# Moving the key and value projections of a decoder layer's attention behind a block of query work

## The chip, the cores and the metric

The kernel runs on one core of a Trainium2 chip. The metric is the device time of one execution in microseconds (us). A core has five engines that run their own instruction streams in order and wait for each other through semaphores: TensorE (PE in the profile; its weight loads are listed as PEld), VectorE (DVE), ScalarE (ACT), GpSimd (POOL) and SyncE (SP). SP does little but issue DMA transfers; ACT issues some too. An instruction that waits holds back all that stands behind it in the same engine's stream.

## The reference

One decoder layer on 1024 tokens of 512 features, in float32. Attention has 32 query heads in 8 groups of four; a group shares one key and one value head of 128 features. Then come a layer norm with the residual, a gated feed-forward network of 1792 hidden features behind an RMS norm, and a second layer norm.

```python
q, k, v = x @ wq, x @ wk, x @ wv             # 32, 8, 8 heads of 128
q = q * cos + rotate_half(q) * sin           # the same for k
scores = einsum('bhtd,bhsd->bhts', q, repeat(k, 4)) / sqrt(128)
att = softmax(where(tril, scores, -inf))
x = layernorm(x + einsum('bhts,bhsd->bhtd', att, repeat(v, 4)) @ wo)
n = rms_norm(x) * ln_w
x = layernorm(x + (silu(n @ gate_w.T) * (n @ up_w.T)) @ down_w.T)
```

## The kernel before, in words

Line numbers (L) are those of the kernel before; the profile names instructions by them. All matmuls are issued in one helper, L145, so the profile tells them apart by their tiles.

**Slots.** Attention is a loop over the groups g = 0 to 7, within a group over eight blocks of 128 tokens in the order i = 7, 1, 5, 3, 4, 2, 6, 0 (p = 0 to 7 counts them), and within a block over four slots of 32 tokens. A slot treats 32 tokens of all four heads at once, so 128 rows, and is named by its place t = 4i + b among the tokens: a group runs through the slots 28 to 31, 4 to 7, 20 to 23, 12 to 15, 16 to 19, 8 to 11, 24 to 27, 0 to 3. `s23` below is the score matmul of slot 23. `scores` (L604) does one slot: TensorE multiplies queries with the keys up to the slot's end (tile `s`, up to two matmuls), VectorE adds the mask and takes the minimum (L623), ScalarE takes the exponential (L643), VectorE the reciprocal of the sum (L647), ScalarE scales (L648), VectorE transposes 32x32 blocks into the tile `turned` (L651). The short slots' remainder is cleared by POOL (L638).

**Behind a block.** After a block's fourth slot `gather` (L683) issues 16 DMAs on SP (L701), which complete the transposition into `moved`. Then, as deferred pieces (`Late`, L816), TensorE multiplies with the values (tile `o`), ScalarE copies (`oT`, L884), and pairs of blocks are multiplied with `wo` in a Strassen scheme: seven products (tile `y`), sums of the operands on POOL (`os`, L785 to L788), sums of the results on VectorE (L807). `y_0` to `y_3` are the four pairs of a group; a pair's last products run in the next group. `load_wo` (L320) issues the two halves of a group's `wo`, `wo_0` and `wo_1`, on SP (L327), when the group before has ended `y_3`; `weigh_wo` (L332) then forms sums of them on POOL (L340 to L343: u1, u3 in place, u2, u4). `y_0` uses `wo_0`, then `wo_1`, then u4, u1, u2 and both halves again.

**Projections.** `project_two` (L492) projects the keys or the values of two groups at a time, or two query heads, for half of the tokens or all, again by seven Strassen products of two matmuls each, which `run` (L975) deals out between slots. `Early` (L900) holds these pieces. What may run at a slot is bounded by a pace (`pace`, `must`) that follows the slot's number, with the constants `KNOWN` and `MOST`. `steps` lists all weight loads in order of use, and `load(s)` issues step s on SP (L249); key weights are scaled by POOL (L258); `weigh(s)` forms sums of the weights on POOL (L293 to L295). Pairs of weights, `wo` halves among them, share four buffers.

**The unit.** In the groups 1 to 5 the queries of the next group (2 to 6, `UNITS`) are projected in one stretch without slots, after p = 4 (`MIDDLE`), by Strassen's scheme nested in itself. This is `Unit` (L1133): seven outer products in the order `INNER` = 1, 2, 6, 7, 5, 3, 4, each a generator `stages` (L1042) with stages that interleave with the neighbours'. A stage ends in ScalarE copies (L1053), and the last in VectorE additions (L1088). `weigh_unit` (L298) forms the outer sums of the query weights on POOL (L306 to L308) and `inner_weights` the inner ones (L1024 on). The sums of the input are kept in HBM and fetched by DMAs that ScalarE issues (`fetch`, L1022; x1, x2, x6 in `prepare` during the four slots of p = 4; x7, x5 at the start of `run`, x3 and x4 within). x6 lies in the part of `turned` that p = 5 to 7 use later. The last stages of the last product run behind the following slots (`ending`). At the end of `run` two loads are issued.

**Rotary work.** A projected query or key tile is rotated later: `rotate_later` (L430) queues three chores, two half multiplications with the sine (L438) and one with the cosine (L443) on VectorE, the last followed by an addition on POOL (L444). `scores` draws one chore per slot.

**Order.** Matmuls, and instructions passed through `ordered` (L1017), keep the program's order on their engine. All others are ordered by a list scheduler, engine by engine, when the kernel is built; the order in which an SP load and a block's gathers come out depends on it.

## Time and profile before

| what | before |
|---|---|
| median of two runs | 1355.7 us (1353.36 and 1358.04) |
| profiled execution | 1354.13 us, span 1352.3 (1.8 us lie around it) |
| mean clock granted to TensorE | 0.972 of full |
| DMA, mean over the span | 102 GB/s, 137.66 MB |
| one SP gather DMA, from issue to landing | about 2.1 us; issues 0.634 us apart |
| `wo` half, query, key, value pair weights, to landing (median) | 5.3, 4.3, 3.9, 3.5 us |
| a unit group's length | about 140.5 us (L145's gaps at 291.78, 431.60, 574.06, 714.73 and 854.01) |

The span is the time from the first to the last instruction. The page's groups give the line, the engine, the operation with its tiles, the shape, the number of instructions, then the busy time and the mean in ns, and last the idle time of the engine ahead of these instructions with what ended most of it ("<-"). A row of the timeline gives the start, the length, the engine, the line, the operation and tiles, how many instructions of one kind follow each other, and, in brackets, the idle time before with its releaser. SPq rows are DMA issues on SP. The table of stretches has, for each window in us: its length, the busy time (and instructions) of PE, PEld, DVE, ACT and POOL, the mean granted clock, the DMA share and GB/s.

### The profile page before, as it was taken

The page shows a single profiled execution, that of the slowest core. Times are in us where ns is not written, and L with a number is a line of the kernel's source. Part 1 is how long each engine was busy: PE and PEld are TensorE (multiplying, and loading weights), DVE is VectorE, ACT ScalarE, POOL GpSimd, SP SyncE. Part 2 cuts the span into 40 slices and gives each one's busy share as a digit, 9 for nine tenths or more (in the row PEclk, how much of TensorE's full clock was granted, in tenths as well). Part 3 has the DMA queues.
Part 4 walks back from the last instruction along what each step waited for, and adds up shares of the span by engine and source line. Part 5 has one row for each costly group of instructions (what it writes and reads, how often), then busy time and mean ns, then how long its engine had stood idle before and what let it go on. Part 6 is the DMA issues. An engine that isn't in the chain of part 4 may idle for free. (4 is left out here: it accounts for less than half of the span.)

```text
span 1352.3 us, 15887 instructions
## 1 busy us (share of the span) xinstructions
PE 1252.4 (93%) x4556; PEld 824.1 (61%) x4556; DVE 966.2 (71%) x1926; ACT 568.2 (42%) x1210; POOL 595.9 (44%) x897
## 2 busy tenths in 40 slices
PE   9999998889988998899898979897999999999998
PEld 5645664655564755555565756554465666886787
DVE  5867885598748863888488747884866577788765
ACT  0443443445334543444344444543546515765100
POOL 5556425342443334234533254333332095969422
PEclk9999999989988998999898999898999999999999
DMA  7344435424552455135622562344354421122000
GB/s 256 68 105 145 130 79 167 137 66 93 145 154 53 99 138 164 55 72 143 183 68 66 127 173 85 75 96 108 91 121 105 115 76 38 42 70 103 2 31 32
DMA packets 90102, 137.66 MB, mean 102 GB/s; under 512 B 18976, under 2 KB 55584, under 8 KB 90016
## 3 DMA queue, kind: packets, MB, share of 16 engines
q1 hardware_dynamic: 83968, 116.33, 33.3%
q10 hardware_dynamic: 6048, 20.32, 4.6%
q8 instruction: 37, 0.61, 0.2%
q14 instruction: 49, 0.40, 0.1%
HBM read 55.58 MB, written 5.77 MB: 45 GB/s over the span
## 5 line engine op out<-in xcount | busy, mean ns | idle before, releaser
L643 ACT ACTIVATE p<-s,low 128x928 f32<-128x928 f32 (+31 forms) x256 | 179.1, 700 | 308.8 <-DVE low L623 276.3
L145 PE MATMUL o<-moved,v 128*128 128x512 f32 x550 | 264.1, 617 | 4.0 <-DVE sums L807 2.0
L623 DVE CUSTOM_DVE_ANT_0 s<-s,mask 128x928 f32<-128x928 f32 (+31 forms) x256 | 179.6, 702 | 93.2 <-PE s L145 92.4
L145 PE MATMUL s<-k,queries 128*128 128x512 f32 (+15 forms) x576 | 206.8, 475 | 36.9 <-ACT p L643 36.9
L648 ACT ACTIVATE p<-p,share 128x928 f32<-128x928 f32 (+31 forms) x256 | 186.5, 734 | 119.0 <-DVE share L647 119.0
L651 DVE STREAM_TRANSPOSE turned<-p 128x1024 f32<-128x1024 f32 (+7 forms) x244 | 184.4, 771 | 60.1 <-ACT p L648 46.3
L145 PEld LDWEIGHTS s<-k,queries 128*128 128x128 f32 x576 | 107.4, 195 | 131.0 <-issue 77.5
L145 PEld LDWEIGHTS o<-moved,v 128*128 128x128 f32 x550 | 107.0, 199 | 113.7 <-issue 101.6
L145 PE MATMUL y<-wo,oT 128*128 128x256 f32 x428 | 108.0, 386 | 10.7 <-DMA wo<-wo 8.0
L444 POOL TENSOR_TENSOR queries<-queries,q_b 128x512 f32<-128x512 f32 x52 | 66.8, 1284 | 92.8 <-DVE queries L443 72.6
L145 PEld LDWEIGHTS y<-wo,oT 128*128 128x128 f32 x428 | 80.7, 193 | 36.6 <-issue 22.7
L638 POOL MEMSET p<- 128x96 f32 (+2 forms) x192 | 26.9, 152 | 166.5 <-DVE turned L651 125.4
L438 DVE TENSOR_TENSOR q_b<-queries,sin 64x512 f32<-64x512 f32 x104 | 94.5, 909 | 3.2
L807 DVE TENSOR_TENSOR sums<-y,sums 128x512 f32<-128x512 f32 x112 | 67.5, 614 | 12.4 <-PE y L145 11.4
L647 DVE RECIPROCAL share<-total 128x1 f32<-128x1 f32 x256 | 39.7, 155 | 44.8 <-ACT p L643 41.4
L884 ACT COPY oT<-o 128x512 f32<-128x512 f32 x58 | 33.7, 580 | 89.1 <-PE o L145 88.9
L145 PE MATMUL s<-kT,queries 128*128 128x512 f32 (+8 forms) x192 | 68.6, 466 | 1.4 <-ACT p L643 1.4
L145 PEld LDWEIGHTS s<-kT,queries 128*128 128x128 f32 x192 | 35.8, 190 | 36.9 <-issue 28.9
L145 PE MATMUL y<-u,os 128*128 128x256 f32 x224 | 54.8, 381 | 1.9 <-POOL os L785 0.8
L145 PE MATMUL a<-x,k 128*128 128x256 f32 x156 | 51.5, 414 | 2.2 <-ACT b L1053 2.2
L643 ACT ACTIVATION_READ_ACCUMULATOR p<-s,low 128x1 f32 x256 | 49.4, 193 | 0.0
L145 PEld LDWEIGHTS y<-u,os 128*128 128x128 f32 x224 | 42.1, 190 | 11.2 <-issue 3.1
(398 smaller groups left out, 2317.8 us busy)
## 6 DMA issues: line engine op xcount, KB each, us to landing
x<-inner_x ACTq DMA_DIRECT2D x30, 512.0 KB, 4.7
moved<-turned SPq DMA_DIRECT2D x112, 128.0 KB, 2.4
moved<-turned SPq DMA_DIRECT2D x128, 112.0 KB, 2.2
moved<-turned SPq DMA_DIRECT2D x112, 96.0 KB, 2.2
moved<-turned SPq DMA_DIRECT2D x112, 80.0 KB, 3.8
wo<-wo SPq DMA_DIRECT2D x16, 512.0 KB, 5.3
moved<-turned SPq DMA_DIRECT2D x128, 64.0 KB, 2.0
wq<-wq SPq DMA_DIRECT2D x14, 512.0 KB, 4.3
```

The costliest lines, as they stand in the source:

```text
L145: tc.keep_in_program_order(nc.tensor.matmul(*args, **kw))
L438: nc.vector.tensor_tensor(alike(b[0], dst)[to], dst[of], alike(sin[:, ts], dst)[of], ALU.mult)
L444: nc.gpsimd.tensor_tensor(dst, dst, alike(b[0], dst), ALU.add)
L623: extreme = nc.vector.tensor_tensor_reduce(out=s[:, :n], in0=s[:, :n], in1=mask[:, T - n :], scale=1.0, scalar=MASKED, op0=ALU.add, op1=AL ...
L638: cleared = nc.gpsimd.memset(p[:, n:full], 0.0)
L643: nc.scalar.activation(p[:, :n], s[:, :n], AF.Exp, bias=low, scale=-1.0, accum_out=total)
L647: nc.vector.reciprocal(share, total)
L648: last_of_all = nc.scalar.activation(p[:, :n], p[:, :n], AF.Copy, scale=share)
L651: nc.vector.transpose(x[:, :, :, b, :].rearrange("p b j q -> p j b q"), p[:, :full].rearrange("p (j b k) -> p j b k", b=B, k=Q),)
L807: pin(nc.vector.tensor_tensor(to, out, to, ALU.add))
L884: nc.scalar.copy(oT, o)
```

## The change

Four things move, all in groups with a unit or next to one.

- The loads: where the group's queries are a unit's, its two loads of query weights are listed ahead of the key or value pair in `steps`; `projections` takes its step accordingly. The unit's end issues the key or value weights and the first query weights of the next unit; `project_two`'s end issues the second, and its last step calls `weigh_unit` for the unit one group on.
- The keys and values of two groups are projected in slots behind the unit (p = 5 to 7) instead of from the group's first slot on. In the first half nothing of `Early` is dealt out (the limit is 0), and the pace in the second counts slots from p = 5, with `KNOWN` 9. `weigh(3 * (g + 1))` stands at p = 5 instead of `weigh(3 * (g + 1) + 1)` at p = 6.
- The unit: the outer products begin at other places, the fetches of x7 and x5 are issued in its first two iterations, and the last product's next-to-last stage runs inside it, so that one stage instead of two is left in `ending`.
- Six rotary chores, those of the first two query heads that the unit has completed, are drawn in its last three iterations (`rotate`), with x6's room as scratch in place of a `rope_b` buffer.

```diff
@@ -96,7 +96,7 @@
 UNITS = range(2, KV - 1)
 UNIT = 24.5
 MIDDLE = 4
-KNOWN = 12
+KNOWN = 9
 INNER = (1, 2, 6, 7, 5, 3, 4)
 
 
@@ -265,8 +265,9 @@
 
         steps = [("v", 0, 1)]
         for g in range(KV - 2):
-            steps.append(("kv"[g % 2], g + 1, g + 2))
-            steps += [("q", 2 * n, 2 * n + 1) for n in (2 * g + 2, 2 * g + 3)]
+            two = ("kv"[g % 2], g + 1, g + 2)
+            four = [("q", 2 * n, 2 * n + 1) for n in (2 * g + 2, 2 * g + 3)]
+            steps += four + [two] if g + 1 in UNITS else [two] + four
         steps += [("k", KV - 1)] + [("q", n, n + 1) for n in (HEADS - 4, HEADS - 2)]
 
         def load(s):
@@ -432,19 +433,24 @@
             ts = slice(even * W, (even + 1) * W)
             b = []
 
-            def half(to, of):
+            def half(to, of, room=None):
+                if not b and room is not None:
+                    b.append(room)
                 if not b:
                     b.append(ap.tile([P, W], F32, tag="rope_b", name=f"{name}_b{even}"))
-                nc.vector.tensor_tensor(
+                return nc.vector.tensor_tensor(
                     alike(b[0], dst)[to], dst[of], alike(sin[:, ts], dst)[of], ALU.mult
                 )
 
-            def whole():
-                nc.vector.tensor_tensor(dst, dst, alike(cos[:, ts], dst), ALU.mult)
+            def whole(room=None):
+                ins = nc.vector.tensor_tensor(dst, dst, alike(cos[:, ts], dst), ALU.mult)
                 nc.gpsimd.tensor_tensor(dst, dst, alike(b[0], dst), ALU.add)
+                return ins
 
             low, high = slice(0, 64), slice(64, P)
-            chores[when].extend([lambda: half(low, high), lambda: half(high, low), whole])
+            chores[when].extend(
+                [lambda room=None: half(low, high, room), lambda room=None: half(high, low, room), whole]
+            )
 
         def chore(behind=None):
 
@@ -571,14 +577,14 @@
                     done(0, 1)
                     if s > 1:
                         load(s + 2)
-                    if s % 3 == 1 and s // 3 + 1 in UNITS:
+                    if s % 3 == 0 and s // 3 + 1 in UNITS:
                         weigh_unit(s // 3 + 1)
                 yield 1
 
         def projections(g):
 
 
-            s, pieces = 3 * (g - 1) + 1, []
+            s, pieces = 3 * (g - 1) + (3 if g in UNITS else 1), []
             if g < KV - 1:
                 pieces.append((PAIR * 2, project_two(s)))
             else:
@@ -1135,7 +1141,7 @@
 
             def __init__(self, g):
                 self.g, self.rooms, self.weights, self.begun = g, {}, [], []
-                self.last = None
+                self.last, self.turns = None, 0
 
             def fetch(self, k, room):
                 self.rooms[k] = room
@@ -1181,6 +1187,14 @@
                     self.v = ap.tile([P, 3, W // 2], F32, tag="os", bufs=1, name=f"v{g}")
                     self.begin()
 
+            def rotate(self, most):
+                room = self.rooms[INNER[2]]
+                for _ in range(most):
+                    if chores[0]:
+                        with_room = (room[:, :W], room[:, W:])[self.turns // 3 % 2]
+                        ordered(chores[0].popleft()(with_room))
+                        self.turns += 1
+
             def begin(self):
                 n = len(self.begun)
                 k = INNER[n]
@@ -1192,28 +1206,37 @@
             def run(self):
                 nonlocal now, quiet
                 g, begun = self.g, self.begun
-                for k in (7, 5):
-                    ordered(self.fetch(k, piece(f"x{k}_{g}")))
                 next(begun[0])
+                self.begin()
                 for n in range(1, len(INNER)):
-                    self.begin()
-                    for back in (1, 0, 2, 1):
-                        if back <= n:
-                            next(begun[n - back])
+                    next(begun[n - 1])
+                    next(begun[n])
+                    if n < 3:
+                        k = INNER[n + 2]
+                        ordered(self.fetch(k, piece(f"x{k}_{g}")))
+                    if n == 1:
+                        self.begin()
+                    if n > 1:
+                        next(begun[n - 2])
+                    next(begun[n - 1])
                     if n > 1 and self.last:
                         self.last()
                         self.last = None
                     self.weigh()
                     if n in (2, 3):
                         ordered(self.fetch(INNER[n + 3], self.rooms[INNER[n - 2]]))
+                    if n > 3:
+                        self.rotate(2)
+                    if 1 < n < len(INNER) - 1:
+                        self.begin()
                 next(begun[-1])
                 next(begun[-2])
-                now += UNIT - 2
+                next(begun[-1])
+                now += UNIT - 1
                 quiet = False
-                ending.extend([begun[-1], begun[-1]])
-                s = 3 * (g - 1) + 1
-                load(s + 3)
-                load(s + 4)
+                ending.append(begun[-1])
+                load(3 * g)
+                load(3 * g + 1)
 
         def step_out(l):
             nonlocal now
@@ -1300,8 +1323,8 @@
                     load_wo(g)
                 if g + 1 in UNITS and p == MIDDLE:
                     unit = Unit(g + 1)
-                if g + 1 in UNITS and p == MIDDLE + 2:
-                    weigh(3 * (g + 1) + 1)
+                if g + 1 in UNITS and p == MIDDLE + 1:
+                    weigh(3 * (g + 1))
                 if g == 0 and p >= NT // 2:
                     for k in INNER[2 * p - NT :][: 2]:
                         with tc.issue_after(cleared.ins):
@@ -1342,10 +1365,12 @@
                         continue
                     end_some()
                     if g + 1 in UNITS and p <= MIDDLE:
-                        pace = early.total * min(1, done / KNOWN)
-                        must = early.total - MOST * max(0, KNOWN + 1 - done)
+                        run(g, due, early, 0, 0, LEAST, 0)
+                    elif g + 1 in UNITS:
+                        behind = done - (MIDDLE + 1) * B
+                        pace = early.total * min(1, behind / KNOWN)
+                        must = early.total - MOST * max(0, KNOWN + 1 - behind)
                         run(g, due, early, pace, must, LEAST)
-                        end_some()
                     elif g < KV - 2:
                         pace = early.total * min(1, passed / (slots - EARLIER))
                         must = early.total - MOST * max(0, slots - EARLIER - done)
```

## The prediction

> **What bounds the kernel now.** First the page: who is busy, and what TensorE waits for.

> ```profile
> PE 1252.4 (93%) x4556; PEld 824.1 (61%) x4556; DVE 966.2 (71%) x1926; ACT 568.2 (42%) x1210; POOL 595.9 (44%) x897
> ...
> L145 PE MATMUL s<-k,queries 128*128 128x512 f32 (+15 forms) x576 | 206.8, 475 | 36.9 <-ACT p L643 36.9
> ...
> L145 PE MATMUL y<-wo,oT 128*128 128x256 f32 x428 | 108.0, 386 | 10.7 <-DMA wo<-wo 8.0
> ```

> TensorE (PE) has 100 us idle in 1352.3, and matmuls run in program order: whatever one of them waits for adds to the time. The change works in groups 1 to 5, which have a unit. TensorE's timeline of one such stretch (group 2, a unit from 373 to 402) shows the gaps in brackets:

> ```profile
> 344.47 1.45 PE L145 MATMUL s<-k,queries 128*128 128x512 f32 x4
> ...
> 356.15 1.89 PE L145 MATMUL y<-wo,oT 128*128 128x256 f32 x8
> ...
> 380.33 1.22 PE L145 MATMUL a<-blocks,wq 128*128 128x256 f32 x2 [4.19 <-ACT a L1053]
> ...
> 406.50 0.67 PE L145 MATMUL ab<-blocks,k 128*128 128x256 f32 x2 [2.09 <-ACT ab L1053]
> ```

> and, 25 us on, at the group's end:

> ```profile
> 431.60 1.17 PE L145 MATMUL s<-k,queries 128*128 128x64 f32 x4 [4.34 <-ACT p L643]
> 432.56 4.57 PE L145 MATMUL o<-moved,v 128*128 128x512 f32 x6
> ...
> 438.46 1.79 PE L145 MATMUL s<-k,queries 128*128 128x512 f32 x4 [1.12 <-ACT p L643]
> ```

> All five groups repeat these: 4.19 at the unit's start, 2.1 at its end, 4.3 + 1.1 in the tail. Idling also costs clock: the six `o` at 432.56 take 4.57, where six take 2.74 at 902.11: 1.8 more, with the scores beside them some 2.6 (estimate). Busy times by stretch (PE, PEld, DVE, then ACT, POOL, granted clock) give the tail's cause:

> ```profile
> 348.40:362.00 13.60, 11.86 (x40) 7.08 (x39) 13.26 (x29) 6.68 (x14) 9.83 (x10) 1.00 0.69 203
> ...
> 425.40:438.40 13.00, 7.61 (x19) 3.99 (x18) 12.49 (x25) 5.85 (x15) 3.25 (x6) 0.74 0.15 36
> ```

> In the last 13 us of a group VectorE (DVE) is full, TensorE is not. That is the stretch to which key/value products move. The price of what else moves is in group 6, where both `wo` loads stand behind gathers on SyncE (SP); first SP's queue in groups 2 and 6, then TensorE in group 6:

> ```profile
> 346.82 1.23 SPq L327 DMA_DIRECT2D wo<-wo  x2
> 352.57 13.66 SPq L701 DMA_DIRECT2D moved<-turned  x16
> ```

> ```profile
> 917.43 4.40 SPq L701 DMA_DIRECT2D moved<-turned  x7
> 921.93 1.06 SPq L327 DMA_DIRECT2D wo<-wo  x2
> ```

> ```profile
> 904.69 1.45 PE L145 MATMUL s<-k,queries 128*128 128x512 f32 x4
> ...
> 925.90 2.04 PE L145 MATMUL y<-wo,oT 128*128 128x256 f32 x4 [8.05 <-DMA wo<-wo]
> ...
> 931.14 1.07 PE L145 MATMUL y<-u,oT 128*128 128x256 f32 x4
> ```

> **Part by part**, per unit group unless said otherwise; positive is slower.

> (1) `wo_1` behind p2's gathers. The built program's SP order, alike in groups 1 to 5, is now wo_0, p2's 16 gathers, wo_1; both loads led before. TensorE's order there is unchanged but for the key/value products: s23, the rest of y_3, s12 to s15, then y_0 with wo_0, with wo_1, with u4. The first gather can't leave before slot 23 is transposed, s23 + 6.4; 16 at 0.634 apart are 10.1; with 0.7 between, SP reaches wo_1 at s23 + 17.2. Group 6 did it in 17.2 (904.69 to 921.93). Landing takes 3.9 (group 6's first, 925.77) to 5.5 (group 2's second, 347.68 to 353.22): s23 + 21.1 to 22.7. TensorE is there at 10.7 (the 11.7 of before, less 1.0 of work that has left the stretch), so it stalls 10.4 to 12.0. Then u4 waits for POOL's three sums L341 to L343, 4.1 in group 6 (927.06 to 931.14); the remaining five products take 5 x 0.86 = 4.3; the clock adds 2 to 2.6. With a landing at 21.4, nearer group 6's, s23 to y_0's end takes 21.4 + 4.1 + 4.3 + 2 = 31.8, of it 15.9 work: 15.9 lost. Before it was 18.7 with 16.8 of work: 1.9 lost. **+14**. Ends: 10 (group 6's row, 8.05 idle, with 2.6 of clock and 1.3 more of u4, less 1.9), and 18 (SP held 4.3 longer, as amid p2's gathers at 360.75 by a fetch of x). In group 6 more work covered the load (TensorE arrived at s23 + 13.2), so I stay in the middle.

> (2) The tail takes seven kv products (12.5 us of PE). TensorE's 7.61 + 12.5 exceeds VectorE's 12.49 plus their few evictions, spread from slot 24 on. Of 5.46 idle and 2.6 of clock (8.1) some 1.5 stays where VectorE is late slot by slot: **-6.6**; ends -8.1 (all goes) and -3 (VectorE, 9.20 of 11.0 busy in the 11 us before, bounds those too).

> (3) The head loses this filler. From s31 (315.53) to o_7 (337.50) were 22.0 us, 21.5 of them work; 8.2 were k products. The 13.3 left don't reach o_7's data: p0's gathers begin 7.7 after s31 (323.23), take 10.1 and land in 2.1: 19.9. That would be 6.6 idle against 0.5. VectorE, 19.43 of these 22.0 busy, loses the evictions of these products and may transpose sooner: **+4.5**, ends 2.5 and 7. What the products hid, the gathers' way, is late now.

> (4) Unit start: the fetches of x7 and x5 no longer stand on ScalarE between slot 19's scale (378.24) and the copy (379.52) that TensorE awaits: 1.3 of the 4.19, **-1.3**; ends -4.2 and 0 (x6's fetch now stands before slot 18's scale, and ScalarE would wait there for p3's gathers). x7 and x5, issued later, land in 4.7 by the page's median, which the stages between them nearly cover: **+0.5**, ends 0 and 3.8 (as late as x6's whole landing, 377.57 to 381.07, plus its issue).

> (5) Unit end: its last stage's copy is no longer awaited behind two slots: **-2.1**. Six rotary steps, 2 x (2 x 0.69 + 0.73) = 4.2, go to VectorE within the unit, 9.11 busy of 20.6 there: nothing; if that cover failed, 4.2.

> (6) Two of the five boundaries (groups 2 and 4, keys): the subtractions for the next unit (POOL, L306 to 308) now stand before the rotary add of the key tile that s28 reads, and wait for a `wq` load that SP holds until the last k product frees its buffer (SP's next gathers wait behind it, but are read 16 us later). POOL then has three sums, a query add, memsets, the key add: 0.5 + 4.4 landing + 3 x 1.27 + 2 x 1.28 + 0.33 = 11.6, against 5.6 of TensorE work in between: **+6 each**, ends 0 and 10. For values nothing reads the late tiles for 20 slots: 0.

> (7) Group 6, once: its `wo` loads now precede p2's gathers; 8.05 and 2.6 go: **-10**. New `kv` loads at the unit's end have 10.9 us to the first product, and need 4.5 + 1.05 + 2.2: 0.

> Sum: 14 - 6.6 + 4.5 - 1.3 + 0.5 - 2.1 = 9.0; x 5 = 45; + 12 - 10 = **+47**. The profiled execution took 1354.1 (span 1352.3): 1401; the median is 1.6 higher: **1402**.

> [...] In before, the clock of 373 to 381 is 0.82 after 4.19 idle, and `o` lost 1.8 after 4.34; but two of the five unit starts ran at full speed after the same 4.19. [...]

> **Rivals.** (a) The stall is covered: p2's gathers pass SP fast enough for wo_1. Then (2) to (5) remain, -5.0 x 5, with (6) at half, 6 in all, and (7): 1354 - 25 + 6 - 10 = 1325, the median **1327**, faster. No change is reached with 5.8 lost a group, which is wo_1 landed at s23 + 13.2: issued at 9, 16 gathers in 2.5 us. The 0.634 spacing of every gather speaks against it; for it, only that SP might stand less long at p2's transposes now that VectorE has less to do there. (b) Stall 10, head 2.5, the boundary 0 to 6: 3.0 x 5 - 10 = 5, to 17: **1361 to 1373**, within 2%. For it: VectorE's 13.26 of 13.6, so that TensorE may arrive later anyway. (c) ScalarE waits for x6's fetch (4.2 a group) and the boundary costs 10: 13.2 x 5 + 20 - 10 = 76, **1432**. For it: that fetch needs p3's gathers, which ended at 377.7. (d) The unit doesn't become what the change says: its ends and fetches gain nothing, 11.9 x 5 + 2 = 62: **1417**.

> **How the numbers follow.** Forecast 0.52, (a) 0.05, (b) 0.17, (c) 0.14, (d) 0.12. A measurement tells 2% from no change, 27 us: 1329 to 1383. Only (a) is faster, (b) the same, the others slower: 0.05, 0.17, 0.78. All low ends together would give 1335, all high ones near 1490; independent ones some 35 to each side: **1364 to 1438**, which takes in (c), (d) and the upper half of (b).

> **What would show it.** TensorE's row of `y<-wo,oT` would carry some 55 us behind `wo<-wo`, five gaps of 10 to 12 at y_0; the 8.05 would be gone; 4.34 and 1.12 mostly gone; a new 4 to 6 ahead of o_7; 4.19 near 3; 2.1 gone; two gaps before s28 that end with POOL's rotary add. No gap at y_0 makes the prediction wrong, by 14 a group; a tail still full of waits does so upward.

## The result, and the profile after

The changed kernel takes 1443.0 us (1442.92 and 1443.09), the one before 1355.7: a ratio of 1.064 (95% interval 1.057 to 1.072). Its profiled execution took 1443.1 (span 1441.3) where that of before took 1354.1: 89.0 us more. The direction was forecast, the size not: 1402 was expected, and the range ended at 1438.

The rows of the page of the changed kernel that answer to those of before (busy and mean, idle time before, its main releaser at the end):

```profile
PE 1280.7 (89%) x4556; PEld 832.8 (58%) x4556; DVE 965.9 (67%) x1926; ACT 563.5 (39%) x1210; POOL 608.0 (42%) x897
...
L145 PE MATMUL s<-k,queries 128*128 128x512 f32 (+15 forms) x576 | 215.8, 491 | 47.7 <-ACT p L649 34.2
...
L145 PE MATMUL y<-wo,oT 128*128 128x256 f32 x428 | 113.4, 398 | 60.9 <-DMA wo<-wo 60.2
```

Two things are to be seen. The wait of `y` for `wo` has grown from 8.0 to 60.2 us. And the same 4556 matmuls are busy 28.3 us longer (1280.7 against 1252.4). By the clock records 20.3 of that is busy time lost at half clock (47.3 against 27.0); the granted clock is 0.944 of full on the mean, and was 0.972. The rest of the 89.0, 60.7, is idle time.

TensorE's timeline in group 2 of the changed kernel, from o_7 through y_0 and the unit to s28 of group 3:

```profile
350.30 8.78 PE L145 MATMUL o<-moved,v 128*128 128x512 f32 x16 [3.85 <-DMA moved<-turned]
358.91 1.45 PE L145 MATMUL s<-k,queries 128*128 128x512 f32 x4
...
381.57 2.07 PE L145 MATMUL y<-wo,oT 128*128 128x256 f32 x4 [10.87 <-DMA wo<-wo]
385.48 2.08 PE L145 MATMUL y<-u,oT 128*128 128x256 f32 x4 [1.83 <-POOL u L344]
...
407.64 0.70 PE L145 MATMUL a<-blocks,wq 128*128 128x256 f32 x2 [2.74 <-ACT a L1059]
...
437.16 0.86 PE L145 MATMUL s<-k,queries 128*128 128x352 f32 x2 [1.53 <-ACT p L649]
...
474.45 3.46 PE L145 MATMUL s<-k,queries 128*128 128x512 f32 x4 [6.80 <-POOL p L644]
```

The four instructions of `y` from 381.57 on run at half speed (2.07 in place of the 1.03 at 362.62), and so does s28 behind the gap of 6.80 (3.46; s28 of group 2 took 1.72); the granted clock is 0.50 at both. The memset that this last row names (L644) is the POOL instruction behind the key tile's rotary addition, which was the late one. SP's queue shows why y_0 waited:

```profile
363.68 0.37 SPq L328 DMA_DIRECT2D wo<-wo  x1
364.71 12.35 SPq L707 DMA_DIRECT2D moved<-turned  x16
377.16 0.53 SPq L328 DMA_DIRECT2D wo<-wo  x1
```

wo_1 left 18.3 us after s23 (17.2 were expected) and landed at 381.52, 22.6 after it (21.1 to 22.7 expected). TensorE had been there at 370.7, 11.8 after s23 (10.7 expected).

To find the 89 us, cut a group at the starts of s28, s20, s23, s16, s8, s24 and s0. The table of stretches gives length and busy time of TensorE; here are four stretches of group 2 of before (s28 to s20, s20 to s23, s23 to s16, and s0 to s28), and then the same of the changed kernel (length, PE, PEld, DVE, ACT, POOL, granted clock, DMA share, GB/s):

```profile
298.59:328.11 29.52, 29.52 (x89) 16.63 (x90) 25.31 (x55) 14.48 (x28) 10.03 (x16) 1.00 0.38 87
328.11:344.47 16.36, 15.86 (x51) 9.25 (x50) 11.67 (x22) 6.58 (x13) 5.53 (x10) 1.00 0.51 118
344.47:363.21 18.74, 17.00 (x59) 10.85 (x58) 16.75 (x33) 8.26 (x17) 11.04 (x13) 1.00 0.59 164
...
426.95:438.46 11.51, 6.06 (x15) 3.23 (x14) 11.06 (x23) 5.23 (x13) 3.14 (x5) 0.70 0.12 28
```

```profile
312.31:338.98 26.67, 24.85 (x85) 15.55 (x84) 22.01 (x45) 13.17 (x26) 13.76 (x19) 1.00 0.27 61
338.98:358.91 19.93, 15.46 (x42) 8.00 (x42) 7.99 (x20) 6.75 (x14) 2.12 (x9) 0.91 0.55 126
358.91:392.71 33.80, 20.14 (x61) 13.63 (x60) 11.18 (x26) 8.22 (x17) 12.98 (x23) 0.75 0.51 140
...
456.21:474.45 18.24, 10.16 (x35) 5.64 (x33) 16.84 (x35) 5.67 (x16) 9.78 (x11) 0.87 0.54 130
```

Since work moves between stretches, lengths alone don't compare. So for each stretch I take the **time lost**: idle time, plus busy time beyond what its matmuls need at 0.43 us per 512 columns, their rate at full clock (the unit's pairs of 128x256 in group 2 begin 0.43 apart from 424.14 to 425.87). Summed over groups 1 to 5 (idle + clock), worked out from the trace (of the 21.6 and 20.5 of clock below, 16.7 and 17.5 are busy time lost in the records of half clock):

| stretch | before | after | more | forecast |
|---|---|---|---|---|
| s28 to s23, the head | 2.4 + 2.4 | 26.4 + 21.6 | +43.2 | (3): +22.5 |
| s23 to s16, y_0 | 11.3 + 3.4 | 69.4 + 20.5 | +75.2 | (1): +70 |
| s16 to s8, the unit | 28.6 + 16.8 | 19.5 + 14.1 | -11.8 | (4): -4 |
| s8 to s24, behind the unit | 10.6 + 1.0 | 6.8 + 2.8 | -2.0 | (5): -10.5 |
| s24 to s28, tail and boundary | 26.7 + 15.4 | 20.1 + 5.6 | -16.5 | (2), (6): -33 + 12 |
| group 6 | 10.1 + 3.8 | 7.3 + 3.0 | -3.7 | (7): -10 |
| groups 0 and 7, the rest | | | +4.4 | 0 |
| sum | | | +88.8 | +47 |

The head is the largest miss, 20.7 over its forecast and half of the 41.8 by which the sum is over; 19.2 of what it added stands in the clock column, though not all of that is time (below). The stall at y_0, the tail and the boundary are near their sizes; the gains behind the unit (8.5 short) and in group 6 (6.3 short) came to a fraction, the unit gained 7.8 more than forecast, and groups 0 and 7 with the rest lost 4.4 for which there was no term.

### The profile page after: what moved, and what is told of

It reads as the page before. It is cut to its first block, busy times and chain, and to the rows that moved or that the text cites. A ratio compares the mean times of both kernels' runs of the same rounds, so it can differ in the third digit from the quotient of the medians.

```text
span 1441.3 us, 15922 instructions
## 1 busy us (share of the span) xinstructions
PE 1280.7 (89%) x4556; PEld 832.8 (58%) x4556; DVE 965.9 (67%) x1926; ACT 563.5 (39%) x1210; POOL 608.0 (42%) x897
## 5 line engine op out<-in xcount | busy, mean ns | idle before, releaser
L649 ACT ACTIVATE p<-s,low 128x928 f32<-128x928 f32 (+31 forms) x256 | 178.7, 698 | 388.5 <-DVE low L629 367.1
L145 PE MATMUL o<-moved,v 128*128 128x512 f32 x550 | 255.4, 602 | 9.3 <-DMA moved<-turned 4.5
L145 PE MATMUL s<-k,queries 128*128 128x512 f32 (+15 forms) x576 | 215.8, 491 | 47.7 <-ACT p L649 34.2
L145 PEld LDWEIGHTS s<-k,queries 128*128 128x128 f32 x576 | 107.8, 197 | 153.6 <-issue 76.2
L145 PEld LDWEIGHTS o<-moved,v 128*128 128x128 f32 x550 | 103.4, 192 | 116.9 <-issue 106.2
L145 PE MATMUL y<-wo,oT 128*128 128x256 f32 x428 | 113.4, 398 | 60.9 <-DMA wo<-wo 60.2
L145 PEld LDWEIGHTS y<-wo,oT 128*128 128x128 f32 x428 | 82.6, 200 | 86.1 <-DMA wo<-wo 59.4
L447 POOL TENSOR_TENSOR queries<-queries,q_b 128x512 f32<-128x512 f32 x42 | 57.6, 1372 | 69.0 <-DVE queries L446 64.6
L644 POOL MEMSET p<- 128x96 f32 (+2 forms) x192 | 26.6, 151 | 141.1 <-DVE turned L657 118.6
L1041 POOL TENSOR_TENSOR k<-wq 128x128 f32<-128x128 f32 x50 | 26.7, 549 | 128.3 <-PE a L145 127.9
L441 DVE TENSOR_TENSOR q_b<-queries,sin 64x512 f32<-64x512 f32 x84 | 74.7, 889 | 4.3 <-POOL queries L447 1.9
L145 PE MATMUL s<-kT,queries 128*128 128x512 f32 (+8 forms) x192 | 70.4, 476 | 5.7 <-POOL queries L424 4.0
L145 PE MATMUL y<-u,os 128*128 128x256 f32 x224 | 63.3, 430 | 0.5 <-POOL os L791 0.5
L145 PEld LDWEIGHTS s<-kT,queries 128*128 128x128 f32 x192 | 36.1, 193 | 42.2 <-issue 29.2
L145 PEld LDWEIGHTS y<-u,os 128*128 128x128 f32 x224 | 49.6, 223 | 14.2 <-issue 4.5
L145 PE MATMUL a<-x,k 128*128 128x256 f32 x156 | 49.4, 400 | 1.1 <-POOL wq L1034 0.6
```

What stands on the lines that cost most here:

```text
L145: tc.keep_in_program_order(nc.tensor.matmul(*args, **kw))
L441: return nc.vector.tensor_tensor(alike(b[0], dst)[to], dst[of], alike(sin[:, ts], dst)[of], ALU.mult)
L447: nc.gpsimd.tensor_tensor(dst, dst, alike(b[0], dst), ALU.add)
L649: nc.scalar.activation(p[:, :n], s[:, :n], AF.Exp, bias=low, scale=-1.0, accum_out=total)
L1041: ordered(nc.gpsimd.tensor_tensor(to, a, b, op))
```

## The experiments

Times are medians; ratios to the kernel before have their 95% interval in brackets.

### wo_1's place: from both sides

In the changed kernel, the rest of y_3 is issued sooner, which frees the buffers of `wo`:

```diff
+                    if g + 1 in UNITS and p == 2 and b == B - 1:
+                        for l in list(late):
+                            if l.g == g - 1:
+                                step_out(l)
                     probabilities = scores(g, t, kTs[g], x)
```

> The changed kernel, but in groups 1 to 5 the remaining products of the last group's y_3 are issued ahead of s23, so that the buffers of wo are free, and both wo loads stand on SP, before p2's 16 gathers. Nothing is left out. Theory (the stall at y_0 is wo_1's place on SP): s23 to s16 takes again what it took before the change, so 15 us a group less; y_3's products also fill part of the idle ahead of o_7 (3.9 in groups 1, 2 and 4): about 1443 - 75 - 10 = 1358, between 1345 and 1370. Rival (the stall is something else of the new order, such as slots arriving late or the clock): y_0 waits for another thing, and less than a third of it goes: above 1415.

Measured: 1373.5 us, 1.015 (1.012 to 1.019) of before. Both loads stand ahead of p2's gathers, and the row of the page has no wait for `wo` left. SP's queue in group 2, then the row:

```profile
349.81 1.24 SPq L328 DMA_DIRECT2D wo<-wo  x2
356.68 18.73 SPq L707 DMA_DIRECT2D moved<-turned  x26
```

```profile
L145 PE MATMUL y<-wo,oT 128*128 128x256 f32 x428 | 106.2, 382 | 0.7 <-ACT oT L890 0.7
```

From s23 to s16 the five groups lose 14.3 (89.9 before this edit, 14.7 in the kernel before the change). The stall is gone whole, 75 us of it. But the time ends 3.5 above its range. The 10 us that y_3 was to fill in the head didn't come, because I had placed it just behind o_7 and not in its wait; in the profiled execution the head lost 4.3 more than the changed kernel's instead, and the unit 5.7 more.

```profile
337.62 9.57 PE L145 MATMUL o<-moved,v 128*128 128x512 f32 x16 [4.24 <-issue]
```

The other way round, the kernel before with wo_1 behind the gathers and nothing else (`last_gather` holds the last DMA of each block's gather; `issue_after` lets no instruction of its block go ahead of the one named, on that engine):

```diff
-                nc.sync.dma_start(t, wo[h0 : h0 + 2 * HD, :].rearrange("(h p) f -> p h f", p=P))
+                behind = r == 1 and last_gather.get((g, 2))
+                with tc.issue_after(behind.ins) if behind else ExitStack():
+                    nc.sync.dma_start(
+                        t, wo[h0 : h0 + 2 * HD, :].rearrange("(h p) f -> p h f", p=P)
+                    )
```

> The kernel before with one thing of the change alone: in groups 2 to 5 wo_1 stands on SP behind p2's 16 gathers (group 1 keeps its order, wo_1 then stands ahead of them). Theory: four groups lose what the changed kernel loses between s23 and s16, 14 to 15 us each less what the k products there still hide (3): 1356 + 4 x 12 = 1404, between 1396 and 1416. Rival (the loss needs the projections to be gone from the first half): below 1375.

Measured: 1419.8, 1.050 (1.046 to 1.053): 66.5 us for four groups, 16.6 each. The row of the page:

```profile
L145 PE MATMUL y<-wo,oT 128*128 128x256 f32 x428 | 112.9, 397 | 63.1 <-DMA wo<-wo 60.5
```

The place of one DMA in one queue costs all of these 66.5 us. That the k products would still hide 3 of it was wrong: 19.4 to 19.9 are lost between s23 and s16 of those groups, a little more than in the changed kernel. SP's queue tells why: with these products in the stretch, p2's gathers begin 8.1 after s23 (353.18 for 345.07 in group 2), not 5.8 (364.71 for 358.91), so that wo_1 leaves 3 us later too.

### The boundary: the weight sums on POOL

```diff
-                    if s % 3 == 0 and s // 3 + 1 in UNITS:
+                    if s == 3:
                         weigh_unit(s // 3 + 1)
...
+                if g + 1 in UNITS and g > 1 and p == 1:
+                    with tc.issue_after(cleared.ins):
+                        weigh_unit(g + 1)
```

> The changed kernel with the unit's three weight sums on POOL behind the memset of slot 30 in place of their place ahead of the key tile's rotary addition. Theory: the two gaps of 6.8 and 6.5 before s28 of groups 3 and 5 go, and with them the low clock behind them (3 us in each head); but o_7 of these groups then waits for its gathers, as it does in the other groups (3.9 and 2.4 of clock): 1443 - 2 x 6.6 = 1430, between 1423 and 1436. Rival (the key tile is late by itself, from VectorE's rotary work): 1443.

Measured: 1429.1, 13.9 less than the changed kernel, as expected (as ratios to before 1.056, 1.052 to 1.059, after 1.064, whose intervals overlap slightly). The mechanism is only half of the gap, though. TensorE and POOL of this kernel at the first of the two boundaries:

```profile
472.62 2.77 PE L145 MATMUL s<-k,queries 128*128 128x512 f32 x3 [3.23 <-POOL p L644]
```

```profile
471.30 1.26 POOL L447 TENSOR_TENSOR k<-k,k_b 128x512 f32<-128x512 f32 x1 [2.12 <-DVE k L446]
472.50 0.13 POOL L644 MEMSET p<- 128x32 f32 x1
472.58 1.67 POOL L307 TENSOR_TENSOR u<-wq,wq 128x512 f32<-128x512 f32 x1
```

The sums now come behind, and still 3.2 of the 6.8 stay: POOL waited for the key tile's cosine product on VectorE (L446) until 471.3. So some 3.5 of each boundary were the weights' wait, and 3.2 the key tile itself, whose last product is now issued as late as between s1 and s2. The two boundaries give 6.8 of the 13.9; 4.4 more was lost less in the heads, 3.0 of it in group 5, while group 3 lost as much clock as before.

### The head: gathers, or the clock

Four matmuls that nobody reads ahead of o_7:

```diff
+                if i == ORDER[0] and g + 1 in UNITS:
+                    spare_o = mbank(f"spare_o{u}")
+                    for j in range(4):
+                        matmul(
+                            spare_o,
+                            lhsT=vs[g][:, j, :],
+                            rhs=s1.rearrange("p c t -> p (c t)")[:, :W],
+                            start=True,
+                            stop=True,
+                        )
```

> The changed kernel with four matmuls of 128x512 that nobody reads ahead of o_7 in groups 1 to 5 (3.5 us at full clock each time); nothing is left out. Theory (what the head lost beside its idle time is the clock after the gap before o_7): in groups 1, 2 and 4 the gap shrinks from 3.7 to 4.5 down to 1 and the clock's loss in s20 to s23 from 2.4 to under 0.6, at no cost of time for the matmuls; groups 3 and 5, where o_7 did not wait, pay their 3.5 and may gain the 3.0 of clock. In all 1443 - 7 + 1 to 7, about 1440. Rival (the low clock comes from the earlier short gaps or from somewhere else): the loss of 2.4 stays and the time rises to 1445 to 1455.

Measured: 1440.8 (a single time, without an interval). TensorE in group 2:

```profile
346.93 3.60 PE L145 MATMUL spare_o<-blocks,v 128*128 128x512 f32 x8
350.50 7.11 PE L145 MATMUL o<-moved,v 128*128 128x512 f32 x16
```

o_7 starts where it did (350.30 in the changed kernel) and takes 7.11 in place of 8.78. The clock's loss in s20 to s23 of groups 1, 2 and 4 fell from 2.4 to 0.5, 0.7 and 0.5. Only in groups 2 and 4 was that time: their heads got 2.1 and 0.7 shorter, o_7 itself 1.7 and 1.8 (in group 4 the way from s28 to s31 got 0.9 longer). In group 1, whose idle time there lies ahead of s21 and s22 more than ahead of o_7 (1.85, 1.22, 0.67), the head got 0.8 longer, and groups 3 and 5 paid 1.1 and 2.7 for the added work. The five heads together got 1.7 longer, so that 1440.8 met the expected 1440 by luck.

In groups 3 and 5 the clock was low without a gap before o_7 (in group 3 half for 6.8 us from 503.85, in the changed kernel). The two short gaps there got matmuls of the same kind, two ahead of s7 and one ahead of s20 (`idle_products(n, name)` issues n of them into one bank):

```diff
+                    if g + 1 in UNITS and t in {7: 2, 20: 1}:
+                        idle_products({7: 2, 20: 1}[t], f"idle{g}_{t}")
                     probabilities = scores(g, t, kTs[g], x)
```

> The changed kernel with matmuls of 128x512 that nobody reads in the two short gaps of the head, in groups 1 to 5: two ahead of s7, one ahead of s20 (0.86 us each at full clock); nothing is left out. In groups 3 and 5 these gaps are 1.97 and 0.97, and behind them the clock is low although no gap of 3 us is near (3.0 lost in s20 to s23). Theory (the two short gaps together lower the clock): that loss falls below 1.0 in groups 3 and 5, and the 2.4 of groups 1, 2 and 4, which lies behind the gap before o_7, stays: 1443 - 6 = 1437. Rival (the low clock of groups 3 and 5 comes from the gap of 6.8 before s28): the 3.0 stay, 1443 or more.

Measured: 1439.8, 1.062 (1.058 to 1.065). In groups 3 and 5 the clock's loss in s20 to s23 went from 3.0 to 0.8, as the theory has it. But no time was gained there: s28 to s23 takes 46.4 and 46.2 after 46.6 and 46.8, because o_7 now waits for its gathers there too (and 1439.8 isn't told apart from the changed kernel's time, as the intervals overlap):

```profile
510.14 7.11 PE L145 MATMUL o<-moved,v 128*128 128x512 f32 x16 [1.19 <-DMA moved<-turned]
```

So o_7's start is set by p0's gathers in all groups: in the changed kernel and in this one o_7 starts 0.1 to 0.4 us after the last of them has landed, 19.5 to 21.7 after s31 (19.9 was reckoned). No run moved these gathers, so this is read from their landings. Clock lost between s31 and o_7 is then free: five groups lost 11.9 of it there in the changed kernel and 6.0 in this one, and took 100.5 and 100.8 for the way. What is lost ahead of s31 or in o_7 itself costs time.

### Both mends, and what is late next

weigh_later's edit, with y_3 drawn ahead of s21, before o_7:

```diff
+                    if g + 1 in UNITS and p == 2 and b == 1:
+                        for l in list(late):
+                            if l.g == g - 1:
+                                step_out(l)
                     probabilities = scores(g, t, kTs[g], x)
```

> The changed kernel with the weight sums behind the memset of slot 30, as in weigh_later, and with the rest of y_3 drawn one step sooner than in y3_early: ahead of s21, so ahead of o_7 and not behind it. Theory (the head's idle time is the way of p0's gathers, and any work covers it): the stretch from s23 to s16 stays at y3_early's level (14 lost in five groups), and the 4.3 us of y_3 lie in the wait before o_7, so 4 a group and 2.4 of clock less in s20 to s23: 1373 - 14 (weigh_later) - 5 x 4 = 1339, between 1330 and 1355. Rival (the head is bound by VectorE's slots, not by the gathers): y_3 in the gap saves nothing, 1360.

Measured: 1362.6, 1.006 (1.004 to 1.007) of before, which is what the rival gave. Its reason is another one. The head behaved: s20 to s23 lost 9.4 in five groups where y3_early lost 29.0. But from s23 to s16 26.8 were lost and not 14.3. SP of this kernel in group 2, then TensorE:

```profile
322.57 20.64 SPq L707 DMA_DIRECT2D moved<-turned  x32
343.31 1.05 SPq L328 DMA_DIRECT2D wo<-wo  x2
```

```profile
356.65 2.05 PE L145 MATMUL y<-u,oT 128*128 128x256 f32 x4 [3.65 <-POOL p L644]
```

SP is busy with the gathers of p0 and p1 until 343.3, so the loads of `wo` leave only 1.0 after s23, however early their buffers are free, and land at 349.7 and 351.8; with y_3 gone from the stretch TensorE is at y_0 before the sums are formed. Even with both mended, this order of the projections isn't faster than before: what it saves in the tail and at the boundary (42.1 lost in before, 18.8 here, from s24 on) it loses in the head (4.8, 28.4) and at y_0 (14.7, 26.8).

### The unit alone, and group 6

The kernel before with the unit's new order (`run`, `begin`, `rotate`, the late stage and the fetches), all else as before. Against it, the change has these lines more, and those of `steps`, `projections` and the pace:

```diff
-                s = 3 * (g - 1) + 1
-                load(s + 3)
-                load(s + 4)
+                load(3 * g)
+                load(3 * g + 1)
```

> The kernel before with the new order inside the unit alone (outer products begun elsewhere, x7 and x5 fetched later, one late stage in place of two, six rotary chores in the unit); projections and loads as before. By the prediction's steps: 1.3 less at the unit's start, 2.1 at its end, 0.5 more for the fetches, so 2.9 a group: 1341. By the changed kernel's stretches: 2.4 less in the unit, 0.4 behind it: 1342. As six chores also leave the full VectorE in the tail, up to 4 a group more may go: down to 1322. Rival (these gains need the moved projections): 1353 to 1358.

Measured: 1346.8, 0.995 (0.994 to 0.997): 6.5 us, about half of what was expected, so neither theory. From s16 to s8 five groups lose 35.1 in place of 45.4. But the wait behind the unit returns as another one (1.29 at s10 for the 2.09 before), and the tail is as slow as it was, in one gap rather than two:

```profile
407.92 0.86 PE L145 MATMUL s<-k,queries 128*128 128x352 f32 x2 [1.29 <-ACT p L648]
425.20 0.41 PE L145 MATMUL s<-k,queries 128*128 128x32 f32 x2 [0.55 <-ACT p L648]
429.40 0.69 PE L145 MATMUL s<-k,queries 128*128 128x64 f32 x2 [3.79 <-ACT p L648]
```

Six chores done in the unit don't free VectorE in the tail (it is busy 11.65 of the 12.00 from 425 to 437): a slot draws one chore as long as there is one, so later ones take the place.

With this unit, and in group 6 the rest of y_3 issued ahead of s20, so that both `wo` loads precede p2's gathers:

```diff
+                    if g == KV - 2 and p == 2 and b == 0:
+                        for l in list(late):
+                            if l.g == g - 1:
+                                step_out(l)
                     probabilities = scores(g, t, kTs[g], x)
```

> The kernel before with the new order inside the unit (as in unit_alone), and in group 6 the rest of y_3 of group 5 is issued ahead of s20, so that group 6's wo loads stand on SP ahead of p2's gathers. Theory (the same place on SP makes the 8.05 at y_0 in group 6 of before): the stall and the clock behind it go, 8 + 2.4, less 1 of new waits: 1346.8 - 9 = 1338. Rival (in group 6 the wait only moves to the next thing that is late, as the changed kernel's group 6 gained 6.5 there and lost 3 elsewhere): 1343.

Measured: **1332.5**, 0.984 (0.982 to 0.986) of before; more went than the theory's 9, as group 6 takes 108.5 where unit_alone's takes 120.6. It loses nothing between s23 and s16 (10.9 in before), and `y` hardly waits for `wo` any more:

```profile
L145 PE MATMUL y<-wo,oT 128*128 128x256 f32 x428 | 106.6, 382 | 2.7 <-POOL oT L792 2.0
```

Nothing else became late in its place (group 6 is idle 1.0 in all). This kernel beats both, the one before by 1.6%.

Two more runs put unread matmuls into its tail gaps, and the second also into the gap at the unit's start:

```diff
+                    if g + 1 in UNITS and t in {1: 4, 2: 1}:
+                        idle_products({1: 4, 2: 1}[t], g, f"idle{g}_{t}")
                     probabilities = scores(g, t, kTs[g], x)
...
                 next(begun[0])
                 self.begin()
+                idle_products(3, g - 1, f"idle{g}_unit")
```

> unit_and_wo6 (1332.5) with matmuls of 128x512 that nobody reads in the tail's gaps, in groups 1 to 5: four ahead of s1 (gap of 3.8), one ahead of s2 (1.3). Theory (in the tail the clock's loss, 2.5 to 4.0 a group, comes from these gaps, and the clock stays up if they are filled): 1332.5 - 5 x 2.5 = 1320, between 1316 and 1326. Rival (the end of the tail is set by VectorE anyway, so that faster matmuls only wait longer): 1331 to 1336.

> tail_warm with three more of these matmuls in the gap of 2.8 at the unit's start. Theory: the clock's loss between s16 and s8, 1.4 to 3.1 a group, goes too: 8 less than tail_warm, about 1312. Rival (the unit's loss is its wait for ScalarE and the fetches, or the added matmuls come later than planned and take their own time): as tail_warm, or up to 5 more.

Measured: 1331.2 (0.982, 0.979 to 0.985) and 1327.8 (0.979, 0.976 to 0.982). TensorE in the first one's tail:

```profile
425.51 3.68 PE L145 MATMUL idle<-k 128*128 128x512 f32 x8
429.47 0.43 PE L145 MATMUL s<-k,queries 128*128 128x64 f32 x2 [0.28 <-ACT p L660]
```

The clock stays up (s1's two matmuls take 0.43, 0.69 in unit_and_wo6; over the whole run 0.994 was granted, 0.980 there), and s0 to s28 gets 1.3 a group shorter (10.2 for 11.4), not 2.5: s1 still waits for an exponential (0.28), now at full clock. So the clock did what the theory says and the time what the rival says (1331 to 1336); the unit also lost 4.8 more in this run. The second came out between its theory (1312) and its rival: from s16 to s8 its five groups take 3.5 less than the first's. Against unit_and_wo6 the first is no clear gain, and the second, 4.7 less, isn't told apart from it, as the intervals overlap.

## Why the prediction was right in its way and wrong in its size

- (1), the stall at y_0: right. 75.2 measured for 70; wo_1's issue, its landing and the wait of 10.9 to 12.5 came within about 1 us of the working. y3_early takes it away, before_wo1_late makes it alone. Only the clock behind it was short: 3.5 to 4.7 a group, not 2 to 2.6.
- (3), **the step that failed**: "+4.5, ends 2.5 and 7", measured 8.6 a group. Cut the head at s31 and at o_7. Between them, the part that the step works out, 6.3 a group more were lost, about what its own working gave (6.6 idle against 0.5) before it was cut to 4.5 on the argument that VectorE "may transpose sooner". It didn't: p0's first gather left 7.3 to 8.6 after s31 (7.7 in the working), the last one landed 19.2 to 20.5 after it. The other 2.3 a group had no term, although (1) and (2) have one for the clock: 1.7 ahead of s31, mostly the clock behind the boundary's gap (2.8 and 3.0 in groups 3 and 5), and 0.6 from the clock in o_7 (1.7 in groups 2 and 4). Half of the 19.2 of clock, 9.7, lies between s31 and o_7, where it stands in place of the wait and adds nothing. That the idle time summed to +24.0 for 22.5 is luck: the "new 4 to 6 ahead of o_7" were 3.9 and 3.1 in groups 2 and 4, 0.7 in group 1 and nothing in 3 and 5; the rest is waits of single scores for ScalarE's exponential (0.5 to 2.4 each).
- (2) and (6): -16.5 for -21 together. The tail's gaps went as expected (4.34 and 1.12 became 1.2 at most where no key boundary followed, which saved 5.9 to 6.4 for 6.6). A boundary cost 6.5 to 6.8 for 6, but for two reasons, of which the step named one.
- (5): "-2.1", measured -0.4. A gap of 1.1 to 1.5 before s10 took the place of the old one, behind ScalarE's exponential (L649); VectorE is busy 12.93 of 13.19 there (428.75 to 441.94). That the chores in the unit cost nothing held; that they help nothing in the tail unit_alone showed.
- (4): -0.8 forecast with the fetches, measured -2.4. The gap at the start fell to 2.74, by 1.45 for 1.3, and a second one of 0.45 behind it went. The fetches rarely made TensorE wait (0.6 at most). In all 1.8 of the 2.4 is idle time, the rest clock.
- (7): "-10", measured -3.7. The 8.05 went, but the last key pair now waits for its weights on POOL (2.44 at 1000.89) and the last queries for their rotation (4.0). In unit_and_wo6, where the loads of the projections are as before, neither wait came up.

On rivals: (a) is refuted by the row of 60.2. (b) had too small a stall. (c)'s 1432 was nearest in size, by another mechanism: ScalarE's waits at the unit's start shrank (2.74, not more than 4.19). (d) isn't what happened either, as the unit's two gaps did change. What the prediction says of the clock fared badly. Behind the 10.9 to 12.5 of idle time at y_0, 3.5 to 4.7 were lost to it, with a granted clock of 0.61 from 381.6 to 394, and TensorE waits 1.83 more within that time. Nor did two of the five unit starts of before run "at full speed", as the prediction has it: the granted clock is half for 3.4 or 6.8 us at all five, and in groups 1 and 5 it only falls 0.5 and 0.9 us after the first matmul.

## What to carry to other kernels

When an edit moves buffers or their releases, look first at what order this makes among the DMAs that one engine issues in order: one load behind sixteen small DMAs cost 15 us five times (75.2), and the list scheduler put it there although its buffer came free about when the first of them was ready (y_3's end 364.5, first gather 364.7). Work that is moved to cover a wait leaves bare the wait that it covered before (24.0 us more of idle time in the five heads): price that one too, and with it the clock behind it. Clock lost ahead of a wait that lasts anyway was free here: 11.9 and 6.0 were lost between s31 and o_7, and the way took 100.5 and 100.8.

## What the runs showed that was not expected

The clock behind the same gap is not the same. In y3_and_weigh s28 of groups 3 and 5 waits 3.23 and 3.22 us, and then 1.97 and 0.97 follow at s7 and s20. TensorE, group 3 and then group 5:

```profile
443.13 1.82 PE L145 MATMUL s<-k,queries 128*128 128x512 f32 x4 [3.23 <-POOL p L644]
444.80 1.89 PE L145 MATMUL y<-u,os 128*128 128x256 f32 x8
```

```profile
721.86 3.46 PE L145 MATMUL s<-k,queries 128*128 128x512 f32 x4 [3.22 <-POOL p L644]
725.11 3.34 PE L145 MATMUL y<-u,os 128*128 128x256 f32 x8
```

The stretches s28 to s20 and s20 to s23 of the two groups (granted clock third from the end):

```profile
443.13:470.92 27.79, 24.85 (x84) 15.63 (x84) 23.62 (x43) 12.40 (x23) 13.39 (x17) 1.00 0.19 42
470.92:487.49 16.57, 16.57 (x57) 10.58 (x57) 12.39 (x28) 7.00 (x14) 3.52 (x6) 1.00 0.57 129
721.86:752.69 30.83, 27.89 (x85) 17.32 (x85) 22.89 (x43) 12.41 (x23) 13.40 (x17) 0.89 0.18 40
752.69:772.24 19.55, 19.55 (x57) 12.50 (x58) 12.50 (x28) 6.98 (x14) 3.51 (x6) 0.84 0.52 119
```

```profile
437.91:441.32 3.41, 1.99 (x11) 1.44 (x9) 3.33 (x10) 1.37 (x5) 1.47 (x3) 1.00 0.91 210
441.32:444.73 3.41, 1.60 (x4) 0.87 (x5) 3.25 (x6) 0.82 (x4) 2.91 (x3) 1.00 0.77 175
444.73:448.15 3.42, 3.42 (x15) 2.66 (x14) 3.09 (x4) 1.12 (x2) 2.52 (x3) 1.00 0.39 86
...
717.80:721.21 3.41, 0.84 (x4) 0.38 (x3) 3.33 (x8) 0.77 (x3) 1.29 (x4) 1.00 0.78 185
721.21:724.63 3.42, 2.77 (x4) 1.39 (x5) 2.11 (x4) 0.40 (x1) 3.34 (x4) 0.50 0.83 188
```

A point splits group 3's gap, and TensorE is busy about half of either piece (1.99 and 1.60). Most of group 5's gap lies in one piece, busy 0.84 us, and two pieces at half clock follow. The short gaps of the changed kernel fit too: in group 3 the 1.97 ahead of s7 lies whole in one piece, busy 0.43 of the time, and the clock is half in the next:

```profile
500.43:503.85 3.42, 1.46 (x6) 0.59 (x4) 3.36 (x8) 1.64 (x5) 2.70 (x4) 1.00 0.18 38
503.85:507.26 3.41, 2.44 (x5) 1.28 (x5) 2.99 (x11) 2.15 (x7) 2.41 (x6) 0.50 0.95 212
```

These are counts from the traces of this case. No run shifted the points on purpose, so a forecast doesn't know where they will lie: a gap of 2 to 4 us may cost, by an estimate from the gaps of 3.23 and 3.22 above, anything from nothing to 3.4 us beyond itself (half of two pieces of 3.41).
